# A graph layer on one core: row fetches on ScalarE's queue, block transfers in pairs, PSUM copies on VectorE

## The chip, the core and the metric

The kernel runs on one core of a Trainium2 chip. The metric is device time in microseconds of that core, the median of several executions; a shorter time is better. The profile is of one further execution.

## What is computed

A layer of a graph network with 50000 nodes of 160 features (64 scalars, 32 vectors of three) and 1650000 edges that are sorted by their target node. Each edge takes the row of its source node, mixes it with four numbers of the edge and with weights, and the results are summed over the edges of each target:

```python
ss, vv = (s[src], v[src])
e0 = sh[:, 0:1]
e1 = sh[:, 1:4]
dot = jnp.einsum('eui,ei->eu', vv, e1)
out0 = C0 * (ss * e0 @ W1 + dot * INV3 @ W2)
p3 = (ss @ W3)[:, :, None] * e1[:, None, :] * INV3
...
m_agg = jax.ops.segment_sum(m, dst, num_segments=n)
hs = m_agg[:, :MUL0] @ Ws * LIN_S
...
h = jnp.concatenate([hs, hv.reshape(n, 3 * MUL1)], axis=1)
return x + jax.nn.relu(h)
```

The result is added to x again and normalised over each node's features. All weights are linear in the row of the source, so the kernel first sums row times edge number over the edges of a target (four sums per node, one for each edge number) and applies the joined weights afterwards.

## The kernel before

**Units, groups, pairs.** A unit is 128 edges, six units are a group, two groups are a *pair*, ten pairs share one load of edges (`SG` = 20 groups). The loop over 1044 pairs is at L800. An edge that leads from a node to itself is taken out beforehand and treated apart ("own").

**A pair.** `gather` (L314) has GpSimd issue one indirect DMA per unit: 128 rows of `x`, 640 bytes each, into the tile `xg` (pool `rows`, four buffers of a pair each). `spread` (L324) has VectorE make `hot` and `ha`, the matrix that places each edge's four numbers at its target's slot (pool `ops`, three buffers). `group_sums` (L336) multiplies, twelve units of `ha` by `xg`, into the PSUM tile `ps` (two buffers), and VectorE transposes the sums out of it (L349).

**Helped units.** Some units are not gathered by GpSimd but row by row. `HELP` (L70) says that SyncE does it, one unit in 72. `fetch` (L665) loads 32 offsets at a time into SyncE's registers (L671) and issues one DMA of 640 bytes for each row (L676) into `xr` (pool `far`, three buffers); four such batches make a unit. The unit is needed two pairs after its last batch. The offsets `ro` are made by ScalarE (L274).

**Chunks and blocks.** Two pairs are a chunk. `apply_weights` (L575) multiplies its sums with the weights and copies the result from PSUM to `hp` (L581). A block is 128 nodes: `ahead` (L588) loads its rows of `x` and its own-edge numbers, `own` (L609) transposes the rows, copies them from PSUM to `xT` (L617), multiplies and leaves `t`; `block` (L633) adds the chunks and `t`; `norm1` to `norm3` normalise (ScalarE's square root at L193, VectorE's reciprocal at L197), and `do_send` (L733) writes 128 rows out. The PSUM tiles of these steps share two buffers under the tag `misc`. `evict` (L245) says which engine copies from PSUM: ScalarE, as long as it has no part in `HELP`.

**Packs.** 128 stretches of 790 edges are a pack, sixteen in all. A pack reads the raw edges, finds the own-edges (`count`, `mark`, `examine`, `aim`), takes them out by moving the others up in five passes over two halves (`shift`, L496 to L513, for the tile `pra` and then for `prow`), sums the own-edges' numbers (L528) and stores each stretch with DMAs to addresses that are read from registers (`store`, L539). Its steps are a list (L571), of which every pair takes its share (L834 to L842), so that a pack is done by the time it is due; places with None are empty steps.

**The order.** Most engines' queues are set by the framework's scheduler, which moves instructions ahead of others as its own model of their times has it. `manual_schedule` (L799) takes SyncE out of that: SyncE's instructions stand in program order. Work that belongs to a later pair is entered with `after_pair`: `do_root` at p + 5, `do_store` at p + 6, `do_send` at p + 8.

Of the kernel before, what the change touches and what calls it, by code (L numbers as in the profile page):

```python
# [38 lines left out]
F32 = mybir.dt.float32  # L39
# [6 lines left out]
ET = mybir.EngineType  # L46
# [3 lines left out]
P = 128  # L50
MUL0, MUL1 = 64, 32
D = MUL0 + 3 * MUL1
NK = 4
# [13 lines left out]
PG = 2  # L67
SG = 20

HELP = {ET.SP: 72}  # L70
HEAD = 100
RP = 128
RS = 16
KM = 31
# [29 lines left out]
def tile_gnn_resnorm(ctx: ExitStack, tc: tile.TileContext, x, src, dst, attr, W1, W2, W3, W4, W5, Ws, Wv, out, n_edges):  # L104
    nc = tc.nc
    N = x.shape[0]
    NBLK, NB, GA, G, NU, NG, L, NH, NR, FAR = plan(N, n_edges)
# [83 lines left out]
    def norm2(pool, mv, n):  # L191
        rstd = pool.tile([P, 1], F32, name="rstd")
        nc.scalar.activation(rstd[:n], mv[:n, 1:2], AF.Sqrt, bias=eps_t[:n])  # L193
        return rstd

    def norm3(pool, y, mv, rstd, n):
        nc.vector.reciprocal(rstd[:n], rstd[:n])  # L197
        o = pool.tile([P, D], F32, name="o")
        nc.vector.tensor_scalar(o[:n], y[:n], mv[:n, 0:1], rstd[:n], op0=ALU.subtract, op1=ALU.mult)  # L199
        return o  # L200

# [14 lines left out]
    nblocks = math.ceil(N / P)  # L216
# [7 lines left out]

    with tc.tile_pool(name="once", bufs=1) as once, tc.tile_pool(name="raw", bufs=2) as rawp, \
            tc.tile_pool(name="idx", bufs=2) as idxp, tc.tile_pool(name="rows", bufs=4) as rowp, \
            tc.tile_pool(name="far", bufs=3) as farp, \
            tc.tile_pool(name="ops", bufs=3) as op, tc.tile_pool(name="sums", bufs=4) as sump, \
            tc.tile_pool(name="hp", bufs=alive + 4) as hpp, tc.tile_pool(name="node", bufs=3) as np_, \
            tc.tile_pool(name="ahead", bufs=7) as aheadp, \  # L230
            tc.tile_pool(name="psC", bufs=1, space=PSUM) as psC, tc.tile_pool(name="psK", bufs=2, space=PSUM) as psK, \
            tc.tile_pool(name="psP", bufs=1, space=PSUM) as psP, tc.tile_pool(name="psA", bufs=2, space=PSUM) as psA, \
            tc.tile_pool(name="psM", bufs=2, space=PSUM) as psM, ExitStack() as later_pools:
# [8 lines left out]
        dq = nc.sync  # L242
# [115 lines left out]
        def row_start(r):  # L358

            lo, hi = (math.floor(r * L * (1 - 1 / degree)) - 2 * FAR - 2, math.ceil(r * L * (1 - 1 / degree)) + 2 * FAR + 2)  # L360
            return (max(lo, 0), hi if r else 0), (max(math.floor((EH + r * L) / degree) - FAR - 2, 0),
                                                  math.ceil((EH + r * L) / degree) + FAR + 2)

        edges = dram.tile([1, (row_start(NR - 1)[0][1] + L) * C], F32, name="edges")
        selves = dram.tile([1, (row_start(NR - 1)[1][1] + W) * NK], F32, name="selves")
        edge_bytes = edges.bitcast(U8).rearrange("o f -> (o f)")
        self_bytes = selves.bitcast(U8).rearrange("o f -> (o f)")
        rows_stored = [0]
# [39 lines left out]
        def pack(c):  # L408

            r0 = c * RP  # L410
            n = min(RP, NR - r0)
            e0 = EH + r0 * L
            e = slice(e0, e0 + n * L)
            steps, T = [], {}
# [154 lines left out]


            for head, j in [(False, j) for j in range(RS)] + [(True, 0)]:  # L571
                steps += [partial(store, head, j), None, None, None]
            return steps + [stored]

        def apply_weights(at, ng):  # L575
# [8 lines left out]
        def rows_of(b):  # L584
            nb = min(P, N - b * P)
            return nb, slice(b * P, b * P + nb)

        def ahead(b):  # L588

            nb, row = rows_of(b)  # L590
            xt = aheadp.tile([P, D], F32, name="xt")
            dq.dma_start(xt[:nb], x[row, :])

            assert rows_stored[0] == NR or row_start(rows_stored[0])[1][0] >= row.stop
            sa = aheadp.tile([P, NK], F32, name="sa")
            dq.dma_start(sa[:nb], selves[0, row.start * NK:row.stop * NK].rearrange("(n k) -> n k", k=NK))
            return xt, sa

        def nodes(b):

# [32 lines left out]
        def block(b, xt, t, hot2):  # L633
# [3 lines left out]
            for i, c in enumerate(cs):  # L637
# [7 lines left out]
        pairs = [(s, g, min(PG, NG - g, (s + 1) * SG - g)) for s in range(NSC)  # L645
                 for g in range(s * SG, min(NG, (s + 1) * SG), PG)]
        batches, helped = {}, {}
        for h, (eng, period) in enumerate(HELP.items()):
            first = PG * G + h * period // 2
            nbatch = P // ROWS[eng]  # L650
            while True:
                at = [int(first + i * period / nbatch) // (PG * G) for i in range(nbatch)]
                q = at[-1] + 2
                if q >= len(pairs) or pairs[q][2] < PG:
                    break
                s, g, ng = pairs[q]
                u = (g - s * SG + ng) * G - 1 - len(helped.get(q, []))
                helped.setdefault(q, []).insert(0, (eng, h))
                for i, p in enumerate(at):
                    batches.setdefault(p, []).append((eng, h, q, s, u, i))  # L660
                first += period
# [46 lines left out]
        def after_pair(p, f, *args):  # L708
            later.setdefault(p, []).append((f, args))

        hps, of_nodes, resid, rstds, outs = {}, {}, {}, {}, {}
# [4 lines left out]
                of_nodes[b] += (nodes(b),)  # L716

        def do_ahead(b):
            of_nodes[b] = ahead(b)

        def do_own(b):
            of_nodes[b] = own(b, *of_nodes.pop(b))
# [5 lines left out]
            rstds[b] = norm2(np_, resid[b][1], rows_of(b)[0])  # L728

        def do_store(b):  # L730
            outs[b] = norm3(np_, *resid.pop(b), rstds.pop(b), rows_of(b)[0])

        def do_send(b):  # L733
            nb, row = rows_of(b)
            dq.dma_start(out[row, :], outs.pop(b)[:nb])

        def do_cast(s):
            raws[s] = cast(raws[s])
# [56 lines left out]
        for at, bs in zip(complete, after):  # L795
            for b in bs:
                after_pair(max(at - AHEAD, START - 1), do_ahead, b)
                after_pair(max(at - AHEAD + 4, START), do_own, b)
        later_pools.enter_context(tc.manual_schedule(engines={ET.SP}))  # L799
        for p, (s, g, ng) in enumerate(pairs):  # L800
            if p % per == 0 and s + 1 < NSC:
                end = min(NG, (s + 2) * SG) * G * P - EH
                assert end <= 0 or rows_stored[0] == NR or end <= row_start(rows_stored[0])[0][0]
                raws[s + 1] = load(s + 1)
                after_pair(p + 1, do_cast, s + 1)
                after_pair(p + 4, do_place, s + 1)
# [12 lines left out]
            if p == START - 2:  # L819
                with ExitStack() as behind, tc.tile_pool(name="begin", bufs=1) as beginp:  # L820
                    for i in first_ones:
                        behind.enter_context(tc.issue_after(i))
                    weights(beginp, psM)
            if p == START - 1:
                with ExitStack() as behind, tc.tile_pool(name="table", bufs=1) as tablep:
                    for i in first_ones:
                        behind.enter_context(tc.issue_after(i))
                    row_table(tablep)
                nc.gpsimd.iota(place_, pattern=[[1, L]], base=1, channel_multiplier=0,
                               allow_small_or_imprecise_dtypes=True)  # L830
                nc.gpsimd.iota(chunk_, pattern=[[1, NCH]], base=0, channel_multiplier=0,
                               allow_small_or_imprecise_dtypes=True)
                packp = later_pools.enter_context(tc.tile_pool(name="pack", bufs=1))
            if packs and p >= START:  # L834
                todo = math.ceil(len(packs[0]) * min(1, (p + 1 - began) / max(1, due[0] - began)))
                for step in packs[0][done:todo]:
                    if step:
                        step()
                done = todo
                if done == len(packs[0]):  # L840
                    packs.pop(0), due.pop(0)
                    done, began = 0, p + 1  # L842
            if (g + ng) % QG == 0 or g + ng == NG:
                for b in after[c]:
                    after_pair(p + 4, do_block, b)
                    after_pair(p + 5, do_root, b)
                    after_pair(p + 6, do_store, b)
                    after_pair(p + 8, do_send, b)
                after_pair(p + 2, do_weights, c, sums, g + ng - c * QG)
                c += 1  # L850
            for f, args in later.pop(p, []):
                f(*args)
# [16 lines left out]
    with tc.tile_pool(name="up", bufs=1) as up, tc.tile_pool(name="us", bufs=2) as us, tc.For_i(0, once_more, 1):  # L869
# [16 lines left out]
        far = up.tile([PB, 2, CB, nseg], F32, name="far2")  # L886
        for s in range(nseg):
# [7 lines left out]
            for c in range(CB):  # L895
# [3 lines left out]
                at = us.tile([PB, 2, SEG], F32, name="at")  # L899
# [18 lines left out]
    with tc.tile_pool(name="edges2", bufs=2) as ep, tc.tile_pool(name="ops2", bufs=2) as op, \  # L918
            tc.tile_pool(name="node2", bufs=1) as np_, tc.tile_pool(name="psA2", bufs=2, space=PSUM) as psA, \
            tc.tile_pool(name="psF2", bufs=1, space=PSUM) as psF:  # L920
        with tc.For_i(0, blocks, 1) as b:
# [5 lines left out]
            with tc.For_i(u0, u1, GA) as u:  # L927
# [11 lines left out]
                for j in range(GA):  # L939
                    nc.gpsimd.indirect_dma_start(  # L940
                        out=xg[:, j, :], out_offset=None, in_=x,
# [29 lines left out]
            xt = np_.tile([NBLK, D], F32, name="xt2")  # L971
            nc.scalar.dma_start(xt, x[row, :])
            y, mv = norm1(np_, ph, xt, NBLK)
            o = norm3(np_, y, mv, norm2(np_, mv, NBLK), NBLK)
            nc.scalar.dma_start(out[row, :], o[:NBLK])


# [31 lines left out]
```

## Time and profile before

| what | us |
|---|---|
| median of 3 runs (22286.48 to 22337.94) | 22318.73 |
| the profiled execution | 15673.7 |
| its span, first to last instruction | 15671.9 |
| GpSimd busy | 11694.9 (75%) |
| TensorE matmul busy | 8017.6 (51%) |
| VectorE busy | 6239.3 (40%) |
| ScalarE busy | 536.9 (3%) |

The profiled execution is 6645 us shorter than the median of the runs; the profile doesn't show why. Registers, branches, waits and the issuing of DMAs don't count as busy, so SyncE has no row of its own, and ScalarE's issuing is not in its share.

The page slices the span in 40: every slice looks like the next, and there is no start or end phase to speak of.

```profile
POOL 7777777777777777777777777777777777777776
PEclk7777777777777777777777777777777777777777
DMA  3323233332333323333233332323333233332322
```

The digits are tenths of the slice. The DMA engines are busy for three tenths. What SyncE issues is in the page's last part (KB of each beside it):

```profile
xr<-in_x SPq DMA_DIRECT2D x22144, 0.6 KB
edges<-prow SPq DMA_DIRECT2D x1994, 18.5 KB
selves<-mine SPq DMA_DIRECT2D x1992, 0.5 KB
xt<-in_x SPq DMA_DIRECT2D x390, 80.0 KB
out<-o SPq DMA_DIRECT2D x390, 80.0 KB
```

### The profile page before, as it was taken

To read this page: it belongs to the slowest core of one execution; us is meant where nothing else is said; L and a number is where in the kernel's file an instruction comes from. 1 tells how busy PE (TensorE), PEld (TensorE's weight loads), DVE (VectorE), ACT (ScalarE), POOL (GpSimd) and SP (SyncE) were. 2 spreads that over 40 slices of the span, in tenths; PEclk is the share of its full clock that TensorE was granted. 3 is DMA by queue.
4 is the path that set the end of the run, shared out by engine and by line. 5 is a ranking of instruction groups with operands and counts; after the bars stand their busy time and mean duration, and the time that the engine had idled before them with its cause. 6 is when DMAs were issued, how large, how long until landed. Compare 5 with 4: busy or idle time off the path is not lost. (4 is left out here: it accounts for less than half of the span.)

```text
span 15671.9 us, 167279 instructions
## 1 busy us (share of the span) xinstructions
PE 8017.6 (51%) x38505; PEld 7282.8 (46%) x38506; DVE 6239.3 (40%) x11070; ACT 536.9 (3%) x1497; POOL 11694.9 (75%) x12363
## 2 busy tenths in 40 slices
PE   4555544554555455554555544555555454555555
PEld 3444444444444444444444444444444444444444
DVE  5342525225253442524425243352433525234322
ACT  0000000000000000000000000000000000000000
POOL 7777777777777777777777777777777777777776
PEclk7777777777777777777777777777777777777777
DMA  3323233332333323333233332323333233332322
GB/s 80 86 73 83 71 80 77 77 84 73 78 80 78 82 74 79 80 77 83 72 79 79 78 82 74 83 73 77 82 76 83 74 80 78 78 80 72 77 73 65
DMA packets 843237, 1218.89 MB, mean 78 GB/s; under 512 B 300227, under 2 KB 623912, under 8 KB 838262
## 3 DMA queue, kind: packets, MB, share of 16 engines
q0 software_dynamic: 592752, 1012.42, 26.3%
q1 hardware_dynamic: 248058, 194.45, 4.4%
q8 instruction: 323, 5.29, 0.1%
q14 instruction: 664, 5.44, 0.1%
q10 hardware_dynamic: 1440, 1.29, 0.0%
HBM read 1135.77 MB, written 71.40 MB: 77 GB/s over the span
## 5 line engine op out<-in xcount | busy, mean ns | idle before, releaser
L319 POOL DMA_INDIRECT xg<-in_x,si x12349 | 11690.7, 947 | 3931.0 <-issue 3711.2
L343 PE MATMUL ps<-xg,ha 128*128 128x160 f32 x24698 | 5320.9, 393 | 6189.6 <-DMA xg<-in_x,si 5282.4
L343 PEld LDWEIGHTS ps<-xg,ha 128*128 128x128 f32 x24698 | 5085.6, 268 | 6411.6 <-issue 5473.8
L349 DVE STREAM_TRANSPOSE sums<-ps 128x320 f32<-128x320 f32 x1044 | 535.8, 513 | 6026.3 <-PE ps L343 5912.1
L331 DVE TENSOR_TENSOR ha<-hot,pk 128x1536 f32<-128x1536 f32 x1044 | 1802.3, 1727 | 733.6 <-PE ps L343 721.8
L579 PE MATMUL phc<-BWk,sums 128*128 128x160 f32 x5220 | 919.7, 329 | 784.0 <-DVE sums L349 677.7
L579 PEld LDWEIGHTS phc<-BWk,sums 128*128 128x128 f32 x5220 | 822.6, 210 | 859.5 <-DVE sums L349 720.6
L623 PE MATMUL yx<-BWh,xT 80*128 80x320 f32 x3128 | 1010.1, 469 | 175.3 <-ACT xT L617 175.1
L627 DVE TENSOR_SCALAR t<-yx,sa 128x160 f32<-128x160 f32 x391 | 149.7, 383 | 1830.5 <-PE yx L623 1816.7
L623 PEld LDWEIGHTS yx<-BWh,xT 80*128 80x128 f32 x3128 | 599.9, 202 | 472.7 <-ACT xT L617 264.3
L639 PE MATMUL phb<-hp,hot 128*128 128x160 f32 x3474 | 607.6, 324 | 301.4 <-DVE t L629 300.6
L639 PEld LDWEIGHTS phb<-hp,hot 128*128 128x128 f32 x3474 | 539.7, 207 | 397.8 <-issue 391.0
L328 DVE TENSOR_TENSOR hot<-bank,rel 128x384 f32<-128x384 f32 x1044 | 555.1, 546 | 4.0
L629 DVE SCALAR_TENSOR_TENSOR t<-yx,sa,t 128x160 f32<-128x160 f32 x1173 | 448.5, 382 | 134.9 <-PE yx L623 110.1
L617 ACT COPY xT<-ptx 80x256 f32<-80x256 f32 x391 | 143.5, 367 | 10397.8 <-PE ptx L615 10218.3
L511 DVE COPY_PREDICATED prow<-marks,prow 128x2370 f32<-128x2370 int32 (+8 forms) x160 | 443.4, 2771 | 0.6
L511 DVE COPY_PREDICATED pra<-marks,pra 128x1580 f32<-128x1580 int32 (+8 forms) x160 | 304.9, 1905 | 0.0
L605 DVE TENSOR_TENSOR hot<-bank,rr 128x512 f32<-128x512 f32 (+2 forms) x391 | 288.4, 738 | 0.0
L640 DVE TENSOR_TENSOR phb<-phb,t 128x160 f32<-128x160 f32 x391 | 129.8, 332 | 365.4 <-PE phb L639 361.6
L581 ACT COPY hp<-phc 128x160 f32<-128x160 f32 x522 | 149.8, 287 | 2895.3 <-PE phc L579 2864.4
L193 ACT ACTIVATE rstd<-mv,eps_t 128x1 f32<-128x1 f32 x391 | 115.2, 295 | 1739.4 <-DVE mv L188 1694.6
L615 PE MATMUL ptx<-ident,xt 128*80 128x128 f32 (+1 forms) x782 | 159.2, 287 | 0.0
(148 smaller groups left out, 2856.8 us busy)
## 6 DMA issues: line engine op xcount, KB each, us to landing
xr<-in_x SPq DMA_DIRECT2D x22144, 0.6 KB
xg<-in_x,si POOLq DMA_INDIRECT x12349
edges<-prow SPq DMA_DIRECT2D x1994, 18.5 KB
r<-edges SPq DMA_DIRECT2D x99, 360.0 KB
selves<-mine SPq DMA_DIRECT2D x1992, 0.5 KB
xt<-in_x SPq DMA_DIRECT2D x390, 80.0 KB
out<-o SPq DMA_DIRECT2D x390, 80.0 KB
pra<-in_attr SPq DMA_DIRECT2D x15, 1580.0 KB
```

The lines of the kernel that those rows point to most:

```text
L319: got.append(nc.gpsimd.indirect_dma_start(out=xg[:, j, :], out_offset=None, in_=x, in_offset=bass.IndirectOffsetOnAxis(ap=placed[0][:, u + ...
L328: nc.vector.tensor_tensor(hot[:, :n], slotsP[:, 0:W].unsqueeze(1).to_broadcast([P, n, W]), rel[:, u:u + n].unsqueeze(2).to_broadcast([P, n ...
L331: nc.vector.tensor_tensor(ha[:, :n], hot[:, :n].unsqueeze(2).to_broadcast([P, n, NK, W]), pk[:, :, u:u + n].rearrange("p k u -> p u k").un ...
L343: mm = nc.tensor.matmul(ps[:, j // G, :], ha[:, j].rearrange("p k w -> p (k w)"), xr, start=j % G == 0, stop=j % G == G - 1)
L349: nc.vector.transpose(at[:, :, i:i + ng, :].rearrange("p b g w -> p g b w"), ps[:, :ng].rearrange("p g (b f) -> p g b f", f=FB))
L511: nc.vector.copy_predicated(what[:n, a:e], mi[:, r].unsqueeze(2).to_broadcast([n, e - a, what.shape[2]]), what[:n, a + d:e + d])
L579: nc.tensor.matmul(ph[:ng * W], at[:, b, :ng].rearrange("p g w -> p (g w)"), BWk[:, b, :], start=b == 0, stop=b == ND - 1)
L605: nc.vector.tensor_tensor(hot2[:, :len(cs)], slotsP.unsqueeze(1).to_broadcast([P, len(cs), P]), rr[:, :len(cs)].unsqueeze(2).to_broadcast( ...
L615: nc.tensor.transpose(pt[:, i, :nb], xt[:nb, i * H:(i + 1) * H], ident[:nb, :nb])
L623: nc.tensor.matmul(y[:nb], xT[:, i, :nb], BWh[:, i, ks, :], start=i == 0, stop=i == 1)
L629: nc.vector.scalar_tensor_tensor(t[:nb], y[:nb, i], sa[:nb, k:k + 1], t[:nb], op0=ALU.mult, op1=ALU.add)
L639: nc.tensor.matmul(ph[:nb], hot2[:r, i, :nb], hp[:r], start=i == 0, stop=i == len(cs) - 1)
```

## The change

ScalarE, not SyncE, fetches units row by row: one unit in 60, in batches of 16 rows (`ROWS`), and ScalarE's queue now stands in program order too. The unit is needed five pairs after its last batch (two before), the buffers for such units are four. The last ten pairs get none, and a batch isn't put before its offsets are made. `evict` follows from `HELP` (L245, unchanged): the copies from PSUM go to VectorE. Blocks are loaded and written in twos (`BP`, `together`), the output tile has its own pool `outs`, and `do_store` and `do_send` move to p + 8 and p + 10. In the packs the empty steps behind each store are gone.

```diff
-HELP = {ET.SP: 72}
+HELP = {ET.Activation: 60}
 HEAD = 100
+BP = 2
...
-            tc.tile_pool(name="far", bufs=3) as farp, \
+            tc.tile_pool(name="far", bufs=4) as farp, \
...
-            tc.tile_pool(name="ahead", bufs=7) as aheadp, \
+            tc.tile_pool(name="ahead", bufs=5) as aheadp, tc.tile_pool(name="outs", bufs=3) as outp, \
...
             for head, j in [(False, j) for j in range(RS)] + [(True, 0)]:
-                steps += [partial(store, head, j), None, None, None]
+                steps.append(partial(store, head, j))
...
+        def together(b):
+
+            bs = list(range(b // BP * BP, min(nblocks, b // BP * BP + BP)))
+            return bs if all(rows_of(i)[0] == P for i in bs) else [b]
+
+        def ahead(bs):
+
+            nb = rows_of(bs[0])[0]
+            n0, n1 = rows_of(bs[0])[1].start, rows_of(bs[-1])[1].stop
+            xt = aheadp.tile([P, BP, D], F32, name="xt")
+            dq.dma_start(xt[:nb, :len(bs)], x[n0:n1, :].rearrange("(h n) d -> n h d", h=len(bs)))
...
+            return [(xt[:, h], sa[:, h]) for h in range(len(bs))]
...
-                q = at[-1] + 2
-                if q >= len(pairs) or pairs[q][2] < PG:
+                q = at[-1] + 5
+                if q >= len(pairs) - 10:
                     break
                 s, g, ng = pairs[q]
+                at = [max(a, (s - 1) * (SG // PG) + 2) for a in at]
...
         def do_ahead(b):
-            of_nodes[b] = ahead(b)
+            bs = together(b)
+            if b == bs[0]:
+                of_nodes.update(zip(bs, ahead(bs)))
...
         def do_send(b):
-            nb, row = rows_of(b)
-            dq.dma_start(out[row, :], outs.pop(b)[:nb])
+            bs = together(b)
+            if b == bs[-1]:
+                n0, n1 = rows_of(bs[0])[1].start, rows_of(b)[1].stop
+                dq.dma_start(out[n0:n1, :].rearrange("(h n) d -> n h d", h=len(bs)),
+                             outs.pop(bs[0])[:rows_of(b)[0], :len(bs)])
...
-        later_pools.enter_context(tc.manual_schedule(engines={ET.SP}))
+        later_pools.enter_context(tc.manual_schedule(engines={ET.SP, ET.Activation}))
...
-                    after_pair(p + 6, do_store, b)
-                    after_pair(p + 8, do_send, b)
+                    after_pair(p + 8, do_store, b)
+                    after_pair(p + 10, do_send, b)
```

More of the change, by code (lines that the diff above doesn't have):

```diff
@@ L194, in norm2, with norm3 @@
         return rstd
-    def norm3(pool, y, mv, rstd, n):
+    def norm3(o, y, mv, rstd, n):
         nc.vector.reciprocal(rstd[:n], rstd[:n])
-        o = pool.tile([P, D], F32, name="o")
         nc.vector.tensor_scalar(o[:n], y[:n], mv[:n, 0:1], rstd[:n], op0=ALU.subtract, op1=ALU.mult)
@@ L586, in rows_of @@
             return nb, slice(b * P, b * P + nb)
-        def ahead(b):
-            nb, row = rows_of(b)
[L591 to L597, printed above, removed]
+        def together(b):
[6 more added lines that the diff above has]
+            dq.dma_start(xt[:nb, :len(bs)], x[n0:n1, :].rearrange("(h n) d -> n h d", h=len(bs)))
+            assert rows_stored[0] == NR or row_start(rows_stored[0])[1][0] >= n1
+            sa = aheadp.tile([P, BP, NK], F32, name="sa")
+            dq.dma_start(sa[:nb, :len(bs)],
+                         selves[0, n0 * NK:n1 * NK].rearrange("(h n k) -> n h k", h=len(bs), k=NK))
+            return [(xt[:, h], sa[:, h]) for h in range(len(bs))]
         def nodes(b):
@@ L730, in do_store @@
         def do_store(b):
-            outs[b] = norm3(np_, *resid.pop(b), rstds.pop(b), rows_of(b)[0])
+            bs = together(b)
+            if b == bs[0]:
+                outs[b] = outp.tile([P, BP, D], F32, name="o")
+            norm3(outs[bs[0]][:, b - bs[0]], *resid.pop(b), rstds.pop(b), rows_of(b)[0])
         def do_send(b):
-            nb, row = rows_of(b)
-            dq.dma_start(out[row, :], outs.pop(b)[:nb])
+            bs = together(b)
+            if b == bs[-1]:
+                n0, n1 = rows_of(bs[0])[1].start, rows_of(b)[1].stop
+                dq.dma_start(out[n0:n1, :].rearrange("(h n) d -> n h d", h=len(bs)),
+                             outs.pop(bs[0])[:rows_of(b)[0], :len(bs)])
         def do_cast(s):
@@ L973, in tile_gnn_resnorm @@
             y, mv = norm1(np_, ph, xt, NBLK)
[L974 removed]
+            o = np_.tile([P, D], F32, name="o")
+            norm3(o, y, mv, norm2(np_, mv, NBLK), NBLK)
             nc.scalar.dma_start(out[row, :], o[:NBLK])
```

## The prediction

> **What bounds the kernel now.** The cores view comes first: one core, span 15671.9 us; the execution it was taken from counts 15673.7 us, so 1.8 us lie around the span. Then the page's groups, the waits, and the timeline of single queues.
>
> ```profile
> L319 POOL DMA_INDIRECT xg<-in_x,si x12349 | 11690.7, 947 | 3931.0 <-issue 3711.2
> L343 PE MATMUL ps<-xg,ha 128*128 128x160 f32 x24698 | 5320.9, 393 | 6189.6 <-DMA xg<-in_x,si 5282.4
> L349 DVE STREAM_TRANSPOSE sums<-ps 128x320 f32<-128x320 f32 x1044 | 535.8, 513 | 6026.3 <-PE ps L343 5912.1
> ```
>
> GpSimd issues 12349 gathers of 128 rows. One takes 0.947 us and 0.30 us of issue stand before it. The timeline shows a start every 1.25 us, and 12349 x 1.25 = 15436 us of the 15672. TensorE idles for the gathers and VectorE idles for TensorE, so both have spare time on average. What GpSimd loses beyond its own rhythm is in the waits view:
>
> ```profile
> POOL xg L319 <- issue: 3711.2, 12175, 0.6
> POOL xg L319 <- PE ps L343: 165.5, 25, 23.2
> ```
>
> 165 us in 25 waits until TensorE is done with an `xg` buffer; fifteen of these last 3.7 to 23.2 us, and they come once per pack (some 900 us). One of them, in GpSimd's queue and in the transposes of VectorE:
>
> ```profile
> 2716.58 0.95 POOL L319 DMA_INDIRECT xg<-in_x,si  x1 [0.30 <-issue]
> 2731.58 0.94 POOL L319 DMA_INDIRECT xg<-in_x,si  x1 [14.06 <-PE ps L343]
> ...
> 2636.24 0.52 DVE L349 STREAM_TRANSPOSE sums<-ps 128x320 f32<-128x320 f32 x1 [13.06 <-PE ps L343]
> 2670.07 0.52 DVE L349 STREAM_TRANSPOSE sums<-ps 128x320 f32<-128x320 f32 x1 [1.59 <-PE phc L579]
> 2706.89 0.51 DVE L349 STREAM_TRANSPOSE sums<-ps 128x320 f32<-128x320 f32 x1
> 2731.34 0.52 DVE L349 STREAM_TRANSPOSE sums<-ps 128x320 f32<-128x320 f32 x1 [2.61 <-PE ps L343]
> ```
>
> Between the first and third transpose lie 70.7 us in which VectorE works through the moves of a pack. TensorE gets no free PSUM tile (`ps`, two buffers) before the next transpose, so `xg` (four buffers) fills and GpSimd stops. A pair of groups is 12 gathers, 15.0 us: VectorE has one transpose per 15 us to give, and a block of pack work between two of them is covered only by GpSimd's lead. The row fetches are no limit: TensorE's `xr` matmuls (346 records) never wait for them.
>
> [...] The trace agrees that the engines are not the limit: q0 takes 26.3% of them, q1 4.4%. [...] The nearest row, L640 on 160 elements in PSUM, shows 0.332 us.
>
> **The change part by part.**
>
> *Fewer gathers.* Before, 22144 / 128 = 173 units go row by row; the changed program has 26240 row DMAs, 205 units. So 32 gathers fewer: 32 x 1.25 = 40 us off the bound.
>
> *Rows on ScalarE.* SyncE's 32 rows take 10.34 us (0.323 each) in its queue, the register load (L671) 2.16 us; a load of 16 registers (L546) 1.23. A batch of 16 on ScalarE is then 1.4 (with its gaps) + 16 x 0.323 = 6.6 us, a unit of eight 52.6 us. A period is 59 gathers, 73.6 us. ScalarE keeps 537 - 150 - 143 = 244 us of its own work, 1.2 us per unit, so it is three quarters full. That ScalarE issues as fast as SyncE isn't shown; it becomes a limit only at (73.6 - 1.2 - 8 x 1.4) / 128 = 0.48 us a row. I take 0.323, no cost; the cover is five pairs, 75 us. In program order `rstd` (L193, 391 of 0.295) stands among the rows and waits for `mv`; rows queue behind it, then VectorE's reciprocal behind the rows. The store is put at +8 instead of +6, so the slack between is three pairs.
>
> *SyncE.* Loses 22144 rows and 692 loads, about 8.7 ms of queue time; xt, sa and out go from 391 to 196 DMAs each (0.37 to 0.44 us). It bounds nothing; the gain is nothing on the path.
>
> *PSUM copies on VectorE.* [...] Hidden by 15 us per transpose outside the packs; inside a pack they come on top, and are in the count below.
>
> *What the order becomes.* The steps of a pack lose three empty places behind each store, ScalarE's evictions leave, and the scheduler sets VectorE's queue anew. This is the part that decides. I laid the durations of the rows of the page on VectorE's order in both programs and summed between transposes. In the changed one nearly a whole pack stands in one place: ten half-steps for `pra` (0.57 + 0.56 + 0.64 + 0.59 + 1.91 = 4.3 us, 43 in all), ten for `prow` (eight full ones of 5.2, two of 3.3, 48), pick and collect 10, the second half's counts 9, and 20 to 25 of ordinary work. In 15 of 16 packs this is three stretches in a row, of 59 to 69, 10 to 17 and 49 to 66 us, together 125 to 140, mean 132. Before, the same work is in three or four blocks per pack, of 28 to 49 us (58 and 69 in two packs), and three stretches in a row sum to 61 to 92. For the pack shown above this method gives 34.0 + 39.1 = 73.1 where the trace has 70.7, so I scale by 0.967: 127.6 us.
>
> *GpSimd's lead against that.* Let T(k) be the transpose ahead of the block. In the trace GpSimd is then 17 gathers past pair k (18 is the median over all transposes). Pairs k+1 and k+2 can still be multiplied (both PSUM tiles), so GpSimd may issue through pair k+6: 72 - 1 - 17 = 54 gathers, 67 us; pair k+3 follows T(k+1) within that, good for 15 more: 82 us. For the pack above this says that GpSimd stops 82 us after 2636.2; it stopped after 81.3. It goes on when pair k+4 is multiplied. In the changed order the last matmul of that pair stands on TensorE behind an own-block and weights that wait for VectorE's evictions at the end of the third stretch: about 127.6 - 3 = 125 us. Stall 125 - 82 = 43 us; 15 packs: 645. The first pack has one stretch of 90 (87 scaled): 87 + 2 - 67 = 22. Sum 667 us, in place of the 165 of before.
>
> *Sum* against the profiled execution: 15673.7 - 40 - 165 + 667 = 16136, +462 us.
>
> **To the runs shown.** Their median, 22318.73, lies 6645 us above the profiled execution, and nothing in the trace tells why. I carry 462 us over as they are: 22780. Were all parts longer by 22318.7 / 15673.7 = 1.424, they would be 658 us: 22977. Were the gathers alone slower, (22318 - 46 - 165) / 12349 = 1.79 us each, the lead covers more: that is the rival below.
>
> **Rivals.**
> 1. *The longer rhythm covers the block: faster.* Place: GpSimd's queue during a pack. At 1.79 us the free run is (54 + 12) x 1.79 = 118 us against 125; 7 us x 15 = 105 remain, and the old stalls are already gone in the time before. From 125 / 66 = 1.89 us a gather on (or a block under 118 us) nothing remains and only 32 x 1.79 = 57 us are gained: 22261. For it: the unexplained 6645 us would fit on GpSimd, which bounds. Against: profile and program are the same, and 0.947 + 0.30 us don't vary. In between, 22290 to 22370, no difference.
> 2. *ScalarE in order is late.* During a block `rstd` waits for an `mv` that stands inside it, up to 100 us; the rows behind it lose 25 us beyond their 75 us of cover, and TensorE waits: 16 x 25 = 400 us more, 23180. For it: `rstd` already waits 1694.6 us on `mv`, at most 46.4 at once. Against: GpSimd stalls then too, and the spare 20 us per period pay the debt back.
> 3. *SyncE sets the unprofiled time.* 22319 us over about 27800 DMAs is 0.80 us each; ScalarE's 205 units would then cost 128 x 0.80 + 11 = 114 us: 23350, or much less than before if SyncE's waits on `o` (2977.8 us) and not its issues were the cost. Against: the trace has no `xr` wait at all.
>
> **How the numbers follow.** Blocks stall GpSimd, by the absolute or the scaled amount: 0.58. Rival 1: 0.25, of it 0.15 faster, 0.07 the same, 0.03 slower. Rival 2: 0.10. Rival 3: 0.07, of it 0.05 faster. Faster or slower means over 0.2%, 45 us, about what a measurement here tells from no change: faster 0.20, same 0.07, slower 0.73. The forecast is 22780. The range takes rival 1 in at the low end, 22240, and the scaled sum with part of rival 2 at the high end, 23250; the forecast's own range is 22550 to 23050.
>
> **What would show it.** GpSimd's gathers 12317 at the same 947 ns; its waits on `ps` at 500 to 850 us in place of 165, in some sixteen pieces of 25 to 60; transposes 59 to 69 and 49 to 66 us apart once per pack; ScalarE's rows 0.32 us apart; no `xr` wait on TensorE. It is wrong if GpSimd's waits on TensorE stay under 200 us, if rows are more than 0.48 us apart, or if TensorE waits for `xr`.

## The result and the profile after

The changed kernel takes 24622.17 us (median of 4 runs, 24554.9 to 24686.07) beside 22328.33 us of the kernel before: ratio 1.103, 95% interval 1.0989 to 1.1071. It is slower, in the foretold direction and by five times the foretold amount (2294 us against 461), and above the range (22240 to 23250).

The kernel before is met here in two conditions: 22.3 to 22.4 ms as in these runs, and 15.7 ms as in the profile that the prediction was made from; one chip showed both (22354 us, and later 15698), and each comparison of times below stands beside runs of before in its own condition.

Changed kernel, the page's costliest groups (operation, count | busy us, mean ns of one | idle us of the engine before it, and what ended most of it) and the slices of GpSimd and of the DMA engines:

```profile
POOL 5454454444544445444554444445454454444454
DMA  2111111111111111111111111111111111111111
...
L319 POOL DMA_INDIRECT xg<-in_x,si x12317 | 11656.1, 946 | 12960.6 <-PE ps L343 7531.4
L343 PE MATMUL ps<-xg,ha 128*128 128x160 f32 x24634 | 4907.4, 363 | 3824.1 <-DVE sums L349 1945.8
...
L349 DVE STREAM_TRANSPOSE sums<-ps 128x320 f32<-128x320 f32 x1044 | 525.3, 510 | 6786.9 <-remote 4404.4
```

The 32 gathers are gone and one gather costs the same 946 ns. The loss stands in the idle column: GpSimd idles 12960.6 us, evenly over the run. The profile that the prediction was made from has 3931.0, but that is one of the faster condition; in a profile of before in the condition of these runs (shown below) it is 10564.8, so that 2396 us are the change's own. "Remote" means that the profile finds no instruction of this core that ended the wait; the first profile of before had no such wait. The waits view (us in total, times, longest):

```profile
ACT rstd L194 <- DMA xr<-in_x: 14760.2, 268, 167.7
POOL xg L319 <- PE ps L343: 7531.4, 258, 134.6
...
PE ps L343 <- DMA xr<-in_x: 3466.2, 137, 75.2
DVE rstd L198 <- ACT rstd L194: 2714.8, 123, 69.7
```

TensorE waits for rows, 3466.2 us where before has 341.3 in the same condition and none in its first profile, and VectorE's reciprocal waits 2714.8 us (140.2 before) for the square root behind the rows. On the timeline ScalarE's rows take most of the span: from the first to the last of the 26240 rows 24412 of the 24672 us pass, 18070 us of them in 25897 steps from row to row of under 3 us and 6342 us in 342 longer ones, in which the queue mostly stands still.

### The profile page after: what moved, and what is told of

The parts are those of the page before. It is cut to its first block, busy times and chain, and to the rows that moved or that the text cites. A ratio compares the mean times of both kernels' runs of the same rounds, so it can differ in the third digit from the quotient of the medians.

```text
span 24671.8 us, 174976 instructions
## 1 busy us (share of the span) xinstructions
PE 8414.4 (34%) x38505; PEld 7320.4 (30%) x38506; DVE 6613.1 (27%) x11983; ACT 266.2 (1%) x584; POOL 11660.4 (47%) x12331
## 5 line engine op out<-in xcount | busy, mean ns | idle before, releaser
L319 POOL DMA_INDIRECT xg<-in_x,si x12317 | 11656.1, 946 | 12960.6 <-PE ps L343 7531.4
L343 PE MATMUL ps<-xg,ha 128*128 128x160 f32 x24634 | 4907.4, 363 | 3824.1 <-DVE sums L349 1945.8
L343 PEld LDWEIGHTS ps<-xg,ha 128*128 128x128 f32 x24634 | 4625.3, 243 | 4137.9 <-DVE sums L349 2145.3
L630 PE MATMUL yx<-BWh,xT 80*128 80x320 f32 x3128 | 1473.8, 622 | 2094.8 <-DVE xT L624 671.5
L343 PE MATMUL ps<-xr,ha 128*128 128x160 f32 x410 | 169.0, 513 | 5168.8 <-DMA xr<-in_x 3466.2
L579 PE MATMUL phc<-BWk,sums 128*128 128x160 f32 x5220 | 1103.1, 365 | 1980.5 <-DVE y L185 741.5
L579 PEld LDWEIGHTS phc<-BWk,sums 128*128 128x128 f32 x5220 | 984.8, 241 | 2075.1 <-DVE y L185 750.1
L630 PEld LDWEIGHTS yx<-BWh,xT 80*128 80x128 f32 x3128 | 779.6, 268 | 2512.0 <-issue 1579.9
L198 DVE RECIPROCAL rstd<-rstd 128x1 f32<-128x1 f32 x391 | 62.1, 159 | 3198.8 <-ACT rstd L194 2714.8
L646 PE MATMUL phb<-hp,hot 128*128 128x160 f32 x3474 | 749.6, 367 | 482.3 <-DVE t L636 258.9
L624 DVE COPY xT<-ptx 80x256 f32<-80x256 f32 x391 | 161.6, 413 | 1774.3 <-PE ptx L622 1258.9
L581 DVE COPY hp<-phc 128x160 f32<-128x160 f32 x522 | 167.1, 320 | 1102.8 <-remote 737.3
```

The costliest lines, as they stand in the source:

```text
L319: got.append(nc.gpsimd.indirect_dma_start(out=xg[:, j, :], out_offset=None, in_=x, in_offset=bass.IndirectOffsetOnAxis(ap=placed[0][:, u + ...
L343: mm = nc.tensor.matmul(ps[:, j // G, :], ha[:, j].rearrange("p k w -> p (k w)"), xr, start=j % G == 0, stop=j % G == G - 1)
L579: nc.tensor.matmul(ph[:ng * W], at[:, b, :ng].rearrange("p g w -> p (g w)"), BWk[:, b, :], start=b == 0, stop=b == ND - 1)
L581: evict(hp[:ng * W], ph[:ng * W])
L624: evict(xT[:, :, :nb], pt[:, :, :nb])
L630: nc.tensor.matmul(y[:nb], xT[:, i, :nb], BWh[:, i, ks, :], start=i == 0, stop=i == 1)
```

## The experiments

Times in us. "First" is the condition in which before takes 15.68 to 15.71 ms, "second" that of 22.36 ms. "Pauses" are stretches of over 0.6 us between two gathers on GpSimd, counted in a trace of each in the first condition; they sum up what GpSimd loses. Where a kernel was timed more than once, ratio and pauses are of one of these times. In the second condition the same count gives 7003 us before, 9415 changed and 4053 before without rows: there too the change's loss, some 2300 us, lies in the pauses.

| kernel | first | ratio to before | pauses | second | ratio |
|---|---|---|---|---|---|
| before | 15677 to 15707 | 1 | 169 | 22354 | 1 |
| changed | 17144 | 1.0922 (1.0902 to 1.0942) | 1708 | 24601, 24561 | 1.101 (1.0991 to 1.1029) |
| changed, no rows | 15703, 15726 | 1.0017 (1.001 to 1.0024) | 5 | not run | |
| before, no rows | 15706 | 1.0019 (1.0011 to 1.0026) | 4 | 19603 | 0.8774 (0.8756 to 0.8793) |
| changed, one unit in 120 | 15691, 15709 | 1.0009 (1.0 to 1.0018) | 127 | not run | |
| changed, rows on SyncE | 16075, 16105, 16110 | 1.0265 (1.0243 to 1.0287) | 649 | not run | |
| changed, no square root on ScalarE | 16559, 16513 | 1.0521 (1.0498 to 1.0544) | 1067 | not run | |
| rows on SyncE, empty steps back | 15912 | 1.0131 (1.0114 to 1.0148) | 436 | not run | |
| changed, rows ten pairs ahead | 16655 | 1.0605 (1.0587 to 1.0622) | 1189 | not run | |
| rows on SyncE, empty steps back, one unit in 48 | 16128 | 1.0267 (1.025 to 1.0284) | 724 | not run | |

**Without rows, with fewer rows, with rows on SyncE.** Four kernels, all in the first condition:

```diff
-HELP = {ET.Activation: 60}
+HELP = {}
...
-        evict = nc.vector.tensor_copy if ET.Activation in HELP else nc.scalar.copy
+        evict = nc.vector.tensor_copy
```

> The changed kernel without any row fetches: all 12522 units by GpSimd, PSUM copies still on VectorE. Left out is nothing of the result. Theory A (ScalarE's queue of rows sets the time): with the rows gone the gathers bound again, 12522 x 1.25 = 15650 us, plus VectorE's pack blocks by my forecast, 667: about 16300 us in the runs and in the profile alike. Theory B (VectorE's longer blocks and copies are the loss, rows only look guilty): 22000 or more stays. Theory C (gathers are slower outside the profile, 1.79 us each): runs at 22400 with a profile of 16300.

Before with `HELP = {}`:

> The kernel before without row fetches: all 12522 units by GpSimd. Theory A (row fetches in a queue set the time of the unprofiled runs of before too, SyncE's rows then): runs fall from 22320 to about 15650 + 165 + ends = 15850, and the profile says the same. Theory C (the gathers themselves are slow outside the profile): runs stay at or above 22320, up to 12522 x 1.79 = 22400 and the profile is 15850.

Changed with `HELP = {ET.SP: 60}` and `evict = nc.vector.tensor_copy`:

> The changed kernel with its rows (one unit in 60, batches of 32) on SyncE instead of ScalarE, PSUM copies still on VectorE. Theory A1 (ScalarE is the slow or the coupled issuer): the profile falls to 16100 to 16400, TensorE waits for no row, and the runs stand near the kernel before. Theory A2 (rows are dear in whatever queue issues them): the runs are as slow as the kernel after, or by the ratio of row numbers above the kernel before, 22320 x 26240 / 22144 = 26400. Theory B: 16300 in the profile with waits of GpSimd on TensorE of some 700 us.

Changed with `HELP = {ET.Activation: 120}`:

> The changed kernel with one unit in 120 instead of 60 by row on ScalarE: half the rows, half the batches. If the time is ScalarE's time per row (24620 us for 26240 rows, 0.94 each), the rows need about 12300 us, fewer than the gathers' 12420 x 1.25 = 15500, and the gathers bound again: 16000 to 16500. If the time is a loop of rstd, the reciprocal and the write of the blocks, once per block whatever the number of rows, it stays above 20000.

Without rows the changed kernel (15703) is level with before without rows (15706), so copies on VectorE, blocks in twos and the packs without empty steps cost nothing that these runs can tell by themselves. Theory B falls, and my forecast's 667 us aren't there either: without rows in the program the scheduler gives VectorE another order, whose heaviest three stretches in a row between transposes hold under 40 us of work a pack on the mean (counted in the trace). With rows on SyncE, in batches of 32 and not 16, the time is 16075, near the 16136 of my sum against the first profile. That is in part luck, as the rows are on another engine there and the stretches are shorter than forecast (below). One unit in 120 on ScalarE costs nothing, although TensorE waits 769 us for rows in it: the waits don't reach GpSimd, whose pauses are no longer than before's (127 us against 169). These said nothing of the 22.3 ms, as before took 15677 beside them; so the same kernels were run again.

**The condition of the first runs.** The changed kernel once more, then before, changed and before without rows beside one another:

> The changed kernel as it is, timed again beside the kernel before, which took 15677 us beside the first four experiments and not 22320. Theory A1 (ScalarE's queue of rows is slow or coupled whatever the condition of the chip): about 24600 again, with TensorE waiting for rows, while before stays at 15677. Theory D (both first times fell under a condition that makes a queue's row issues slow, on SyncE in before and on ScalarE after): 15700 to 16400, the rows 0.33 us apart on the mean too. Period 120 took 15691, so by A1 the limit lies between one unit in 120 and one in 60.

> The kernel before as it is, for its profile under the condition of its runs. Beside the kernels with one time of 15677 its profile showed rows on SyncE 0.341 us apart on the mean. Where its runs take 22360, theory D (a queue's instructions become slow, as ScalarE's do in the profile of after: multiples of 0.70 us for an instruction in stretches that sum to a third of the time) expects the same stretches on SyncE, rows 0.7 or more apart on the mean, TensorE waiting for rows, and gathers at the same 0.947 us. Theory C (gathers slower) expects gathers at 1.3 us or more. Where its runs take 15677, it repeats the first profile.

> The changed kernel beside the one above. Where before takes 22360: 24600 again. Where before takes 15677, theory D (slow issues under a condition of the chip make the whole loss) expects 15700 to 16200, rows 0.34 us apart on the mean and GpSimd's waits on TensorE of 150 to 700 us; theory A1 (ScalarE's order and its semaphores make the loss whatever the condition) expects over 20000.

> The kernel before without row fetches, a second time, beside the two above. Where before takes 22360, theory D expects 15700, as no queue issues rows: the kernel without helped units would win by 30% there. Theory C expects 22400. Where before takes 15677 it is 15706 again.

Before took 22360 both times, the changed kernel 24601 and 24561, before without rows 19603. With before slow beside it, the changed kernel's slowness could not part theory A1 from theory D. But this gave the missing profile. Before in the second condition, groups and waits:

```profile
L319 POOL DMA_INDIRECT xg<-in_x,si x12349 | 11686.3, 946 | 10564.8 <-PE ps L343 4990.0 <-issue 3625.8 <-remote 1486.6
...
L349 DVE STREAM_TRANSPOSE sums<-ps 128x320 f32<-128x320 f32 x1044 | 536.5, 514 | 7819.1 <-remote 6618.9 <-PE ps L343 834.1 <-issue 308.3
```

The gathers cost the same, so theory C (slower gathers) falls. SyncE's queue on the timeline (start, us, count of rows), two batches of 32, and the same two stretches in the windows view (busy us and count of each engine, clock, DMA share, GB/s):

```profile
4132.99 32.91 SPq L676 DMA_DIRECT2D xr<-in_x  x32
...
4633.67 10.82 SPq L676 DMA_DIRECT2D xr<-in_x  x32
```

```profile
4133.00:4166.00 33.00, 11.41 (x40) 9.91 (x39) 2.50 (x3) 0.37 (x1) 21.69 (x24) 0.60 0.24 59
4633.60:4644.30 10.70, 7.37 (x18) 4.96 (x18) 2.87 (x9) 0.66 (x2) 0.00 (x0) 0.50 0.01 3
```

The fifth pair of numbers is GpSimd: 24 gathers beside the batch of 32.91 us, none beside that of 10.82. Over all batches, from the first row's start to the last one's end, the medians are 32.9 us where GpSimd starts gathers at four fifths or more of its rate of one per 1.25 us (295 batches) and 10.7 us where it starts none (141). In the profile of the first condition a batch takes 10.4 us beside GpSimd at that rate (678 batches):

```profile
4172.59 10.33 SPq L676 DMA_DIRECT2D xr<-in_x  x32
```

So in the second condition SyncE's batches take three times as long while GpSimd gathers (32.9 us against 10.7), and VectorE did three operations in the 33 us above, nine in the 10.7. GpSimd's waits for TensorE (4990.0 us in 220 waits, against 165.5 in 25 in the first condition) fit with this: it runs until its buffers are full, then waits until the others have caught up. Theory D holds for rows, but is too narrow: without rows 19603 and not 15700 remain, 3897 us more than in the first condition, so the greater part of the 6647 us between the conditions of before isn't the rows'. Whether the issuing of gathers or their traffic slows the others (the DMA engines are busy for 0.24 of one stretch and 0.01 of the other), and why the condition is there, no run shows.

**The square root off ScalarE.** VectorE makes `mv` + eps, and the root is left out:

```diff
-        nc.scalar.activation(rstd[:n], mv[:n, 1:2], AF.Sqrt, bias=eps_t[:n])
+        nc.vector.tensor_scalar(rstd[:n], mv[:n, 1:2], EPS * HALF * HALF, None, op0=ALU.add)
```

> The changed kernel with nothing on ScalarE beside the rows: VectorE makes mv + eps in place of ScalarE's square root, and the square root itself is left out of the computation. Then no row waits for mv, and the reciprocal waits for no row; the semaphores that rows share with SyncE's writes of o stay. Theory L (the loop rows, rstd, reciprocal, write of o, rows makes a good part of the loss): the long waits between rows (6300 us in all in the profile of after) shrink to under 1500 and the time falls by 3000 or more where before takes 22360. Theory S (slow instructions alone: 26240 rows at 0.70 us on the mean and 1640 register loads fill ScalarE's queue): 24000 or more stays. Where before takes 15677: within 300 us of it if rows are cheap there, as I think.

Beside it the three kernels from above again:

> The changed kernel without row fetches, again. It took 15703 where before took 15677. Where before takes 22360: the kernel before without rows took 19603 there. If the other parts of the change (blocks in twos, copies on VectorE, no empty steps) cost nothing, 19000 to 19700, and all of the loss against before comes from rows on ScalarE. If they are a part of the loss, over 20000.

> The changed kernel with its rows on SyncE, one unit in 60, again. It took 16075 where before took 15677. Where before takes 22360: if rows cost by their number in whatever queue, 22360 plus 4096 rows x 0.9 us of queue = up to 26000; if ScalarE is the worse queue for them, 22300 to 23300.

> The changed kernel with one unit in 120 on ScalarE, again. It took 15691 where before took 15677. Where before takes 22360: ScalarE's queue then needs about 12300 of the 24600 us, and the time is that of the kernel without rows, 19000 to 19700, if the rows' queue alone makes the loss. If every row slows the other engines in proportion, half way: about 22000.

All four fell in the first condition, where they repeat the times above (15726, 16105, 15709) or give 16559; what they were to show of the second stays open. The changed kernel, beside two of these kernels and in the first condition too, gave the missing comparison:

> The changed kernel as it is. Where before takes 22360: 24600, known. Where before takes 15680: rows there cost 0.34 to 0.37 us, and the kernel with the square root off ScalarE took 16559. Theory L (the loop of rows, rstd, reciprocal and write of o costs beside the rest) expects 16700 to 17500 with ScalarE's queue waiting over 5000 us in pieces of more than 3 us; my forecast's theory (VectorE's pack blocks alone) expects 16136.

> The changed kernel with its rows on SyncE, one unit in 60. It took 16075 and 16105 where before took 15680. Where before takes 22360: if rows cost by their number in whatever queue, up to 26000; if ScalarE is the worse queue for them, 22300 to 23300.

> The changed kernel with the square root left out and VectorE's mv + eps in its place, so that ScalarE has nothing beside the rows and their offsets. It took 16559 where before took 15698. Where before takes 22360: theory L (the loop is a good part of the loss there) expects 21600 or less; theory S (slow instructions fill ScalarE's queue by themselves) 24000 or more.

So in the first condition the change costs 17144 - 15695 = 1449 us: 415 stay with rows on SyncE (16110), 403 more come with rows on ScalarE alone (16513), and 631 with the square root among them (17144). Theory A1 is right that ScalarE is the worse place for rows, but its "over 20000" for this condition missed, as did theory D's 15700 to 16200. Theory L's 16700 to 17500 came, with ScalarE's queue standing for 5233 us. Its other sign for this condition didn't: without the root the kernel isn't within 300 us of before but 818 off. And ScalarE's queue, whose long waits the theory expected to shrink to under a quarter (where before is slow), still stands for 4546 us without the root. The changed kernel in the first condition, waits view, then SyncE's own queue, then SyncE's queue with the rows on SyncE:

```profile
ACT rstd L194 <- DMA xr<-in_x: 11396.3, 309, 138.1
...
PE ps L343 <- DMA xr<-in_x: 1539.7, 106, 43.6
...
POOL xg L319 <- PE ps L343: 1496.2, 70, 66.2
DVE rstd L198 <- ACT rstd L194: 1369.7, 121, 43.8
...
PE ptx L622 <- DMA xt<-in_x: 882.9, 49, 65.9
PE pk L301 <- DMA r<-edges: 755.4, 68, 30.2
```

```profile
SPq L750 <- DMA xr<-in_x: 6936.8, 130, 180.1
SPq L563 <- DMA xr<-in_x: 3521.9, 1263, 14.7
SPq L750 <- DVE y L185: 2318.7, 106, 58.0
SPq L750 <- DVE o L199: 1555.7, 27, 117.0
```

```profile
SPq L563 <- DMA edges<-prow: 156.9, 359, 1.3
```

The write of `o` (L750) and the packs' stores (L563) share no data with the rows, yet wait for them. The events in the trace say why: the DMAs of SyncE and ScalarE take eight semaphores in turn (3907 or 3908 DMAs on each), and each waits for the one before it on the same semaphore, whichever queue that was in: in the changed kernel's profile of the second condition 30560 of the 31259 wait on their own semaphore, and 4702 come next on it after one of the other queue. Such a wait holds the queue here: in the profile of the first condition ScalarE issues nothing for up to 115.3 us while its next row waits for a write of SyncE's.

Not each of these waits costs time. Of what the write of `o` waits for rows, all but 10 us lie before `o` itself is written, so the 6936.8 us cost next to nothing; the stores' 3521.9 us do put off what stands behind them. The dear waits go the other way, and the waits view, which leaves out ScalarE's issuing, doesn't list them: 110 times, 3437 us in all, a row stands behind a write of `o`, and for 3196 us of this VectorE hasn't made `o` yet. The write goes out as soon as `o` is there, the row 2.1 us later (medians).

With the root this makes a circle: rows wait for SyncE's writes, these for VectorE's `o`, that for `rstd` on ScalarE, and `rstd` for the rows ahead of it. Leaving the root out opens the circle. VectorE's 1369.7 us of waits for `rstd` and 631 us of the time are gone, but rows still stand 3175 us behind writes (114 times) and TensorE waits longer for rows (2617.2 us) than with it. So the circle explains 631 us. The 403 us without it come with rows on ScalarE, but no run tells the shared semaphores, the smaller batches and SyncE's late loads apart; that the semaphores are the link is read from the traces and was not tried by taking them apart. In the second condition the same links show in the changed kernel (VectorE 2714.8 us for `rstd`, TensorE 3466.2 us for rows), but no kernel that opens them was met there.

One stand on ScalarE's timeline:

```profile
5925.74 5.72 ACTq L684 DMA_DIRECT2D xr<-in_x  x16
5931.50 0.29 ACT L194 ACTIVATE rstd<-mv,eps_t 128x1 f32<-128x1 f32 x1 [22.57 <-DMA xr<-in_x]
5999.31 0.43 ACT L274 ACTIVATE ro<-r 120x128 int32<-120x128 f32 x1 [67.51 <-DMA r<-edges]
6001.16 8.91 ACTq L684 DMA_DIRECT2D xr<-in_x  x22
```

This batch takes 5.72 us, and over all batches a row follows the last after 0.36 us on the mean (0.33 on SyncE): issuing is nearly as cheap as on SyncE. Then the queue stands 67.5 us for the offsets `ro`, whose edges `r` SyncE loads only at 5998, after a run of stores. The same run holds up a block's `xt`, loaded at 5978, and TensorE stands for it; then `r`. This, more than ScalarE's own stand, is what GpSimd waits for here:

```profile
5980.31 0.65 PE L622 MATMUL ptx<-ident,xt 128*80 128x128 f32 x2 [46.25 <-DMA xt<-in_x]
...
6009.95 0.95 POOL L319 DMA_INDIRECT xg<-in_x,si  x1 [37.24 <-PE ps L343]
```

Over the run TensorE waits 882.9 us for `xt` and 755.4 for `r`, as much as for rows; with the rows on SyncE it is 3.3 us for `r` and nothing for `xt`. ScalarE's queue stands 5233 us in 174 pieces of over 3 us in this run, 3437 of them for the writes of `o` and 1221 before `ro`. Issuing the rows from a further engine cost 1034 us here, by 16110 against 17144.

**The rest, and a better mixture.**

```diff
-                steps.append(partial(store, head, j))
+                steps += [partial(store, head, j), None, None, None]
```

in the kernel with rows on SyncE, then the same with `HELP = {ET.SP: 48}`, and in the changed kernel, apart from these:

```diff
-            tc.tile_pool(name="far", bufs=4) as farp, \
+            tc.tile_pool(name="far", bufs=6) as farp, \
...
-                q = at[-1] + 5
+                q = at[-1] + 10
```

> The changed kernel with its rows on SyncE (one unit in 60) and with the three empty steps behind each store of a pack put back. With rows on SyncE alone it is 16110 where before takes 15695, and GpSimd has sixteen gaps of 32 to 58 us, one in each pack. Theory O1 (the packs' steps, drawn together, make VectorE's blocks): the gaps fall to those of before (165 us in all) or less, and the time to 15640 to 15750. Theory O2 (the PSUM copies on VectorE or the blocks in twos make them): 16000 or more stays.

> The changed kernel with rows on ScalarE asked for ten pairs ahead instead of five, six buffers instead of four. The changed kernel takes 17144 where before takes 15695; 1034 of this is gone with rows on SyncE. Theory L1 (rows come late because ScalarE's queue stands still in pieces of up to a hundred us, but has time enough on the mean): more lead hides it, 16100 to 16400. Theory L2 (the queue stands still because rows, rstd, o and its write wait for one another in a circle, so that ScalarE has no time to spare however early it starts): 16800 to 17300. Where before takes 22360, ScalarE's queue is full and nothing is gained: 24000 to 24700.

> The first of these with one unit in 48 instead of 60 on SyncE: 256 units, 51 more than with 60 and 83 more than before has. GpSimd's gathers bound, 1.25 us each, so 51 fewer are 64 us less than the first of these: 15580 to 15690, under the kernel before, if O1 holds and SyncE keeps up (128 rows x 0.34 and four loads, 52 us, in a period of 60 us). If SyncE is late, TensorE waits for rows and it is slower than the first of these. Where before takes 22360, more rows are more time: over the first of these by 400 or more.

The empty steps explain half of the 415: 15912 against 16110, pauses 436 against 649, and VectorE's three heaviest stretches hold 89 us in place of 101. It missed both theories' numbers; whether copies, twos, the later store or the larger share of rows make the other 200 us wasn't tried.

More lead gave 16655, between both expectations. I split the pauses into those that lie in the sixteen heavy VectorE stretches and the others: 717 and 991 us in the changed kernel, 268 and 921 with more lead, 730 and 338 without the square root, 644 and 6 with rows on SyncE. So nearly all of the gain lies in the heavy stretches, which the scheduler, setting VectorE's queue anew, made shorter (97 us of work in place of 124), and the other pauses stayed: that speaks for theory L2, although its 16800 was missed and TensorE's waits for rows fell from 1539.7 to 805.2 us. Without the root the other pauses fall by 653 us, about the 631 by which the time falls.

One unit in 48 is 216 us slower than one in 60: SyncE's queue is late again (TensorE waits 786.4 us for the edges `r` and 292.5 for rows) and the pauses grow from 436 to 724 us. No kernel beat before in the first condition. Of those run in the second only before without rows did, by 12.3%; in the first it costs 0.19%.

## Why the prediction was wrong

*Fewer gathers.* Right: 12317 at 946 to 948 ns; the 40 us are lost in the pauses.

*Rows on ScalarE: "I take 0.323, no cost". This step failed.* The rate was nearly right in the first condition (0.36 us a row, below the limit of 0.48), but the queue wasn't three quarters full of work with a quarter to spare: it stood 5233 us in waits of over 3 us. Rows on ScalarE cost 1034 us there, counted at nothing. Rival 2 named the place, `rstd` among the rows, at 10% and 400 us; I dismissed its size because the spare 20 us per period would pay the debt back. They don't: each stand also delays what the next `rstd`, write or load needs. What neither the sum nor the rivals had is that rows wait for SyncE's writes of `o`, 3437 us.

*SyncE "bounds nothing".* Wrong. It lost 22144 rows, but the rows wait for its writes, its stores wait 3521.9 us for rows that it no longer issues, and the loads behind these come late: TensorE waits 882.9 + 755.4 us for `xt` and `r`.

*PSUM copies on VectorE hidden.* Right where rows are out (15703); beside rows not separated. What a copy costs on VectorE was not shown when I forecast, as before makes these copies on ScalarE; in the changed kernel's profile of the first condition one to `hp` takes 0.32 us and one to `xT` 0.41, in all 522 x 0.32 + 391 x 0.41 = 327 us.

*VectorE's packs.* Near in the first condition, in part by luck. Forecast: three stretches of 127.6 us, 43 us of stall in a pack, 667 in all. In the changed kernel's own profile there the heavy stretches hold 124 us on the mean and 717 us of pauses, 45 a pack. One of them, transposes of VectorE and GpSimd's answer:

```profile
5146.09 0.52 DVE L349 STREAM_TRANSPOSE sums<-ps 128x320 f32<-128x320 f32 x1 [10.41 <-PE ps L343]
5208.95 0.49 DVE L349 STREAM_TRANSPOSE sums<-ps 128x320 f32<-128x320 f32 x1
5218.69 0.50 DVE L349 STREAM_TRANSPOSE sums<-ps 128x320 f32<-128x320 f32 x1
5288.84 0.91 DVE L349 STREAM_TRANSPOSE sums<-ps 128x320 f32<-128x320 f32 x2 [7.21 <-PE ps L343]
...
5295.81 0.94 POOL L319 DMA_INDIRECT xg<-in_x,si  x1 [48.70 <-PE ps L343]
```

62.9, 9.7 and 70.2 us between transposes, against the foretold 59 to 69, 10 to 17 and 49 to 66; GpSimd stands 48.7 us. The packs make some two fifths of the pauses that the change adds (717 - 131 of 1708 - 169; 131 lay in them before), and I took them for all. The step from a stretch's length to its pause (length less 82 us) isn't confirmed: with rows on SyncE the stretches hold 101 us, yet their pauses are 644 us, 40 a pack where that step gives some 20.

*"I carry 462 us over as they are".* This failed too. The 6645 us between profile and runs were another condition of the chip, in which SyncE's and ScalarE's batches are slow while GpSimd gathers (a batch of 32 on SyncE 32.9 us, of 16 on ScalarE 10.3). Against the profile's condition the sum was short by 1019 us (the changed kernel's profiled execution there took 17154.9, forecast 16136), about what rows on ScalarE cost; against that of the runs by 1833. Rival 3 had the resource, queue time per row (0.80 us; measured on ScalarE 0.64 in batches beside gathers and 0.36 in batches beside none), at 7%; its 23350 left the circle out. What the circle and the slow issues cost apart in the second condition stays open, since the kernels that separate them were met in the first only.

Of the signs that I had named, two came: TensorE waits for `xr`, in both conditions, and rows are over 0.48 us apart within a batch in that of the runs (0.63 on the mean, stands left out).

## What to carry to other kernels

Before work goes into another engine's in-order queue, write down for each instruction already there what it waits for, and follow that through every queue to what is moved; a wait for another queue isn't seen in a count of free microseconds. Look for waits between transfers that share no data: here eight semaphores used in turn joined two queues that the program keeps apart, and rows stood 3437 us behind writes. Ask of each such wait what came last: of the 6936.8 us that the write of `o` waited for rows, all but 10 lay before `o` was there and cost next to nothing. And where profile and runs differ by 42%, an absolute cost from the profile isn't a forecast: first find what differs, here by a second profile of the same kernel.

## What the runs showed of the hardware

In one of two conditions that one chip showed (before 22354 us, and later 15698), SyncE's and ScalarE's queues are slow while GpSimd gathers: a batch of 32 row DMAs on SyncE takes 32.9 us beside gathers and 10.7 us while GpSimd stands, against 10.4 us beside gathers in the other condition. On ScalarE a batch of 16 takes 10.3 us beside gathers and 5.7 us without; in the other condition 5.5 and 5.4. Of the register moves between SyncE's rows, 0.03 us as a rule, 3804 of 22144 last over 0.6 us there, most 0.70, and none in the other condition. The gathers themselves take 0.946 us in both. The kernel without rows still loses 19603 - 15706 = 3897 us to it. And two issuing engines that share eight semaphores weren't independent, with the DMA engines mostly free: in the changed kernel of the first condition 110 rows stood 3437 us in all behind writes of the other queue, while the DMA engines were 24% busy with gathers and 4% with the rest.
